# Sums of exponentials taken from a column of ones in v, in a two-layer attention kernel

## The chip, the cores and the metric

The kernel runs on one core of one Trainium2 chip. The metric is device time in microseconds, as the median of several runs. Engines are named as the profile names them: PE multiplies matrices, DVE, ACT and POOL work elementwise, SP only issues DMAs here; ACT and POOL can issue DMAs too.

## The reference

The input is x of shape (4, 32, 32, 768), in float32. Two layers follow one another, each with a residual: `x = x + layer(group_norm(x))`.

- Layer 0 makes q, k and v with three 768 x 768 products, splits them into 12 heads of 64 channels, and attends over the 1024 tokens of an image. Each score gets a bias for relative rows and one for relative columns, both from q. A projection follows.
- Layer 1 makes q, k and v likewise, then runs a 3x3 convolution per channel over each of them, and a layer norm over the 64 channels of a head, with a gain and an offset. Attention with the same kind of bias follows, q is added to its result, and a projection ends the layer.

```python
attn = softmax(q @ k.T * scale + rel_h + rel_w)   # per head, over 1024 keys
o = attn @ v                                      # layer 1: + q
```

The softmax divides by a sum of exponentials over the keys. How that sum is found in layer 1 is what changes. A layer norm's output, ahead of gain and offset, sums to zero over the 64 channels: the last channel is minus the sum of the other 63.

## The kernel before

All tensors lie with channels on the 128 partitions and tokens along the free axis. Two heads share the partitions (64 each) and are handled together as a *pair*; 6 pairs make one layer of one image, called a stage, and 8 stages (images 0 and 1 through layer 0, then through layer 1, then images 2 and 3 the same way) make 48 pairs. A pair's 1024 queries are handled in two *chunks* of 512 (`QC`).

**Attention of a chunk** (`attend`). The keys come in two groups of four tiles of 128. For each tile, PE makes the scores of both heads (L748) and adds the bias by a second product with `ones` (L750), ACT takes the exponential of 128 x 1024 values into `e` (L755). The four score tiles use the banks `ps_a`, `place_b`, `place_c` and `ps_a` again, so the fourth waits for the first one's exponential. After the group, PE multiplies the four `e` with v (`vt`) into `av`, 64 rows for each head (L770). On the side, DVE adds all eight `e` of a chunk into `acc` (L762 for the first two, L764 for the others).

When a chunk's last `av` is done, ACT copies it to SBUF as `weighed` (`copy`, L705). The remaining work is put off by a list, `rest`, and each call of `more()` runs one piece:

- `sums`: PE multiplies `acc` with a block of ones, which leaves each head's sums on all its 64 rows (`z`, L712); ACT copies them to `t` (L719) and finds a reciprocal by Ln and Exp (L721, L722). It comes after the next group's scores.
- `result`: DVE refines the reciprocal (L727, L728) and multiplies `weighed` by it (L731 in layer 1, where L732 applies v's gain and adds q; L734 in layer 0).
- `finish`: in layer 0 ACT adds v's bias.

**The other work** is laid between these groups. The generator `attend` yields 8 times for a chunk, two times after each group's scores and two times after each group's `av`, which makes 16 numbered *steps* for a pair, some 5 us each. A table, `events`, holds pieces of work by step number, written out by hand in `Pair.plan` and at the end of `two_layers`. No scheduler reorders them: each engine runs its instructions in the order in which the pieces were called.

For a pair of layer 1, whose pieces run while the pair before is attended, they are: products for q, k and v (`padded`, L131 `qkv`, with ACT's L515 into padded images), nine taps of the convolution on DVE (`taps`, L530 and L532), centring by a product (`centre`, `ln_c`) with ACT's squares and copies (L545, L546), sums of squares on DVE (`squares`, `lnv`), normalization (`norm`: `ln_ln` and `r_ln` on ACT, `t_ln` and L561 on DVE), transposes back (`back`, `ln_t`) with ACT's writes of `q`, `q_t` (L483, L484) and `k` (L492), and the bias: `positions` (`rel`, L590, copied to `whole` by L595 and L596), then `split`, in which ACT casts `whole` to `high` (L606), DVE takes the rest (L607), and POOL issues 16 DMAs of 128 KB that spread both into `bias` (L617).

In layer 0 most pairs use sevens of block products in place of eights (`sevens`, tiles `m4m2`, `m3m5`, `m1m6`, `m7`). They need sums of weight blocks, which `mix_weights(u)` makes once: it loads two weights by SP (the first of two steps), adds blocks on DVE and writes them to DRAM (`mixed`, the second step). For u of 12, 13 and 14, the projection of layer 1, the second step also finds the product of v's offset with the projection (`pbias`, L281: two groups of six products with a single column each). Token blocks are mixed on DVE by `mix_tokens` (L304). Group norm of the next stage (`gn_mean`, `gmean`, `gn_var`, xn) and the projection of the last one (`p4p2`, `p3p5`, `p1p6`, `p7`, `os_sums`) are further pieces.

**Banks.** `small_bank` gives one bank that all its users share in turn, and `bank` goes round a list (`turn`) of single banks in `place_b` and `place_c` and the small one, set anew after each group.

Of the kernel before, what the change touches and what calls it, by code (L numbers as in the profile page):

```python
# [17 lines left out]
P = 128  # L18
# [5 lines left out]
D = 64  # L24
HALF = T // 2
QC = 512
# [8 lines left out]
NSMALL = 81  # L35


IDENT, GROUP, CENTRE, HEADS, ONES = 0, P, 2 * P, 3 * P, 3 * P + 2
NCONST = 3 * P + 2 + D


LIMIT = 1e15
# [3 lines left out]
def two_layers(ctx: ExitStack, tc: tile.TileContext, keep, x_in, wqkv, wproj, rels, windows, vrow, small, const, onehot, picks, out):  # L46
# [19 lines left out]
    nc = tc.nc  # L66
# [5 lines left out]
    work = pool("work", 2)  # L72
# [52 lines left out]
    def small_bank(name):  # L125
        return ps_small.tile([P, 512], F32, tag="small", name=name)
# [14 lines left out]
    cst = fixed.tile([P, NCONST], F32, tag="cst", name="cst")  # L141
# [8 lines left out]
    def rsqrt(v, n, name):  # L150

        ln = stat.tile([P, n], F32, tag=f"ln{n}", name=f"ln_{name}")
        nc.scalar.activation(ln, v, AF.Ln)
        r = stat.tile([P, n], F32, tag=f"r{n}", name=f"r_{name}")
        nc.scalar.activation(r, ln, AF.Exp, scale=-0.5)
# [107 lines left out]
    def mix_weights(u):  # L263


        a = wp.tile([P, NC, P], F32, tag="wproj", name="mix_a")
        b = wp.tile([P, NC, P], F32, tag="wproj", name="mix_b")
        if u < PROJ_SUMS:
            (pa, sa), (pb, sb) = two(u, 0) if u < V_SUMS else two(2 * (u - V_SUMS), 2)
            nc.sync.dma_start(a, wqkv[0, pa, :, sa])  # L270
            nc.sync.dma_start(b, wqkv[0, pb, :, sb])
        else:
            layer, m = divmod(2 * (u - PROJ_SUMS), NC)
            for i, w in enumerate((a, b)):
                nc.sync.dma_start(w, wproj[layer, :, :, m + i, :].rearrange("h p q -> p h q"))
        yield
        for i, w in enumerate((a, b)):
            if u >= PROJ_SUMS and layer:
                ps = small_bank("pbias")
                for n in range(NC):  # L280
                    nc.tensor.matmul(ps[:, 0:1], w[:, n, :], col(LN + 5), start=(n == 0), stop=(n == NC - 1))  # L281
                nc.vector.tensor_tensor(pbias[:, m + i : m + i + 1], ps[:, 0:1], col(BIAS[1] + 18 + m + i), ALU.add)
# [24 lines left out]
    def group_norm(stage):  # L307

        xn = xns[stage]
        st = stat.tile([P, NC * 2, 6], F32, tag="bn", name="bn", bufs=1)  # L310
        for n in range(NC):
            for h in range(2):
                nc.vector.bn_stats(st[:, 2 * n + h, :], xn[:, n, h * HALF : (h + 1) * HALF])
            if n in (1, 3):
                yield
        mv = stat.tile([P, 2], F32, tag="mv", name="mv")
        nc.vector.bn_aggr(mv, st.rearrange("p a b -> p (a b)"))
        yield
# [5 lines left out]
        nc.vector.tensor_copy(mean, ps[:, 0:1])  # L324
        d = stat.tile([P, 1], F32, tag="gd", name="gd")
        nc.vector.tensor_sub(d, mv[:, 0:1], mean)
        nc.vector.scalar_tensor_tensor(d, d, d, mv[:, 1:2], ALU.mult, ALU.add)
        yield
        yield
        ps = small_bank("gn_var")  # L330
        nc.tensor.matmul(ps[:, 0:1], group, d, start=True, stop=True)
        v = stat.tile([P, 1], F32, tag="gv", name="gv")
        nc.vector.tensor_scalar(v, ps[:, 0:1], EPS, None, ALU.add)
        yield
        r = rsqrt(v, 1, "gn")
        yield
# [26 lines left out]
    class Pair:  # L363
# [189 lines left out]
        def norm(self, s):  # L553
            r = rsqrt(self.v, 2 * NKT, "ln")
            c = self.c[s].rearrange("p (a d) -> p a d", d=D)
            dst = c
            if s == 2:

                self.make_vt()
                dst = self.vt.rearrange("p t (j d) -> p (t j) d", d=D)  # L560
            nc.vector.tensor_tensor(dst, c, r.unsqueeze(2).to_broadcast([P, 2 * NKT, D]), ALU.mult)  # L561

        def back(self, s, h):

# [55 lines left out]
        def plan(self):  # L620

            Q, K, V = 0, 1, 2
            if not self.layer and not in_sevens(self.i):
                return [
                    (0, lambda: self.plain(Q, 0)),
                    (2, lambda: self.plain(Q, 1)),
                    (4, lambda: self.plain(K, 0)),
                    (5, lambda: self.positions(0)),
                    (6, lambda: self.plain(K, 1)),
                    (7, lambda: self.positions(1)),  # L630
                    (8, lambda: self.plain_v(0)),
                    (10, lambda: self.split()),
                    (10, lambda: self.plain_v(1)),
                ]
            if not self.layer:
# [51 lines left out]
    def attend(pair, os):  # L687
# [12 lines left out]
        for c in range(T // QC):  # L700
            cols = slice(c * QC, (c + 1) * QC)

            def copy(av):
                weighed = one.tile([P, QC], F32, tag="weighed", name="weighed")
                nc.scalar.copy(weighed, av)  # L705
                return weighed

            def sums(weighed, acc, c=c):

                z = small_bank("z")  # L710
                for j in range(2):
                    nc.tensor.matmul(  # L712
                        z[j * D : (j + 1) * D, :], cst[:, ONES : ONES + D], acc[:, j, :],
                        start=True, stop=True,
                    )
                at = 2 * (pair.i * (T // QC) + c)
                t = work.tile([P, QC], F32, tag="t", name="t", bufs=1)
                inv = work.tile([P, QC], F32, tag="inv", name="inv", bufs=1)
                nc.scalar.activation(t, z, AF.Copy, accum_out=seen[:, at : at + 1])  # L719

                nc.scalar.activation(inv, t, AF.Ln, bias=tiny)  # L721
                nc.scalar.activation(inv, inv, AF.Exp, scale=-1.0, accum_out=seen[:, at + 1 : at + 2])  # L722
                return weighed, t, inv
# [18 lines left out]
            for g in range(0, NKT, 4):  # L742
# [32 lines left out]
                more()  # L775
                if g + 4 == NKT:
                    rest.extend((sums, result, finish))
                    found = (copy(av), acc)
                yield
                yield  # L780

# [134 lines left out]

    for u, call, step in (
        (2, 0, 5), (7, 6, 11), (3, 13, 18), (4, 22, 29), (8, 31, 38), (5, 40, 47), (0, 49, 55), (6, 57, 63), (1, 65, 71),
        (9, 72, 77), (10, 78, 83), (11, 84, 89), (12, 138, 143), (13, 145, 150), (14, 152, 157),
    ):  # L920
        mix = mix_weights(u)
        for at_step in (call, step):
            at(at_step, lambda mix=mix: next(mix))
# [281 lines left out]
def _laid_out(inp):  # L1205
# [24 lines left out]
    const[:, CENTRE : CENTRE + P] = eye - head  # L1230
    const[:, HEADS : HEADS + 2] = np.kron(np.eye(2), np.full((D, 1), 1.0 / D))
    const[:, ONES : ONES + D] = 1.0
    key = np.arange(T)
    onehot = np.concatenate([np.arange(S)[:, None] == key // S, np.arange(S)[:, None] == key % S])

# [36 lines left out]
```

## Time and profile before

| | |
|---|---|
| time, median of 3 runs | 3917.45 us (3915.82 to 3919.93) |
| profiled execution, its time | 3920.75 us |
| its span, first to last instruction | 3918.9 us |
| mean granted PE clock | 0.993 |
| L764 and L762, adds into `acc` on DVE | 576 x 1225 ns and 96 x 1224 ns |
| L712, products for `z` on PE | 384 records, 103.6 us |
| L705, L719, L721, L722 on ACT | 96 each, 587, 600, 722 and 631 ns |
| L281, products for `pbias` on PE | 72 records, 12.4 us |
| DMA traffic | 318 MB, 81 GB/s in the mean |

A PE product in float32 shows as two records, each 128x512 one with its partner on the other 64 columns at the same time. Busy time is the union of the records. A line's idle time is that of its engine just before it, with the releaser that ended it. PEclk is the clock that PE was granted, as a share of full speed[...].

### The profile page before, as it was taken

The page shows a single profiled execution, that of the slowest core. Times are in us where ns is not written, and L with a number is a line of the kernel's source. Part 1 is how long each engine was busy: PE and PEld are TensorE (multiplying, and loading weights), DVE is VectorE, ACT ScalarE, POOL GpSimd, SP SyncE. Part 2 cuts the span into 40 slices and gives each one's busy share as a digit, 9 for nine tenths or more (in the row PEclk, how much of TensorE's full clock was granted, in tenths as well). Part 3 has the DMA queues.
Part 4 walks back from the last instruction along what each step waited for, and adds up shares of the span by engine and source line. Part 5 has one row for each costly group of instructions (what it writes and reads, how often), then busy time and mean ns, then how long its engine had stood idle before and what let it go on. Part 6 is the DMA issues. An engine that isn't in the chain of part 4 may idle for free.

```text
span 3918.9 us, 79880 instructions
## 1 busy us (share of the span) xinstructions
PE 3835.0 (98%) x34738; PEld 1726.2 (44%) x34738; DVE 2673.5 (68%) x3088; ACT 1850.3 (47%) x2741; POOL 411.7 (11%) x776
## 2 busy tenths in 40 slices
PE   7999999999999999999899999999999999999998
PEld 3535535534344444444444455355443444434442
DVE  2566454448789988799654554445686898878885
ACT  2455434445345553455533554254553555535551
POOL 0111000110000010000010010011100010000010
PEclk9999999999999999999999999999999999999999
DMA  4344452331331122311144222522115121142112
GB/s 147 102 120 120 127 163 61 94 83 38 105 100 39 39 60 83 115 45 39 41 118 135 56 73 64 167 63 75 42 52 155 35 56 43 39 118 57 36 47 95
DMA packets 184710, 318.11 MB, mean 81 GB/s; under 512 B 24352, under 2 KB 77472, under 8 KB 184352
## 3 DMA queue, kind: packets, MB, share of 16 engines
q1 hardware_dynamic: 122912, 212.19, 17.3%
q0 software_dynamic: 61440, 100.71, 11.2%
q8 instruction: 277, 4.54, 0.5%
q14 instruction: 81, 0.66, 0.1%
HBM read 172.23 MB, written 39.91 MB: 54 GB/s over the span
## 4 chain that ended last, share of the span: by engine, by line
PE 86%; DVE 11%; DMA 1%; issue 1%; ACT 1%; POOL 0%; DVEq 0%; SPq 0%; ACTq 0%
PE qkv L131 18%; PE s L748 15%; PE av L770 15%; PE m4m L131 4%; PE m3m L131 4%; PE m1m L131 4%; PE s L750 4%; DVE shared L532 3%; PE p3p L131 3%; DVE acc L764 3%; PE p1p L131 3%; PE p4p L131 3%; PE ln_c L131 3%; PE rel L590 3%; PE z L712 2%; PE m L131 2%
## 5 line engine op out<-in xcount | busy, mean ns | idle before, releaser
L755 ACT ACTIVATE e<-s 128x1024 f32<-128x1024 f32 x768 | 777.2, 1025 | 412.1 <-PE s L750 379.5
L764 DVE TENSOR_TENSOR acc<-acc,e 128x1024 f32<-128x1024 f32 x576 | 705.5, 1225 | 182.7 <-ACT e L755 132.2
L131 PE MATMUL qkv<-xn,wqkv_t 128*64 128x512 f32 x3648 | 815.8, 596 | 6.8 <-DVE gmean L324 4.1
L748 PE MATMUL s<-q,k 64*128 64x512 f32 x3072 | 817.1, 609 | 4.3 <-ACT e L755 3.5
L532 DVE SCALAR_TENSOR_TENSOR shared<-shared,sm 128x1056 f32<-128x1056 f32 x576 | 758.4, 1317 | 15.0
L750 PE MATMUL s<-bias,ones 64*128 64x512 f32 x1536 | 617.0, 796 | 10.9 <-DMA bias<-high 7.5
L770 PE MATMUL av<-e,vt 128*64 128x512 f32 x2624 | 595.0, 595 | 0.0
L617 POOL DMA_DIRECT2D bias<-high x384 | 203.6, 546 | 3237.8 <-ACT high L606 3003.6
L131 PEld LDWEIGHTS qkv<-xn,wqkv_t 128*64 128x64 f32 x3648 | 254.2, 137 | 491.5 <-issue 481.6
L515 ACT ACTIVATE shared<-qkv,sm 128x512 f32<-128x512 f32 (+1 forms) x288 | 129.3, 502 | 632.7 <-PE qkv L131 632.7
L748 PEld LDWEIGHTS s<-q,k 64*128 64x128 f32 x3072 | 283.2, 188 | 263.2 <-issue 216.8
L770 PEld LDWEIGHTS av<-e,vt 128*64 128x64 f32 x2624 | 185.6, 137 | 347.1 <-issue 322.0
L762 DVE TENSOR_TENSOR acc<-e 128x1024 f32<-128x1024 f32 x96 | 117.5, 1224 | 285.9 <-ACT e L755 280.1
L750 PEld LDWEIGHTS s<-bias,ones 64*128 64x128 f32 x1536 | 150.8, 189 | 199.2 <-issue 191.6
L617 POOL DMA_DIRECT2D bias<-whole x384 | 206.1, 558 | 106.6 <-DVE whole L607 97.0
L705 ACT COPY weighed<-av 128x512 f32<-128x512 f32 x96 | 56.4, 587 | 279.3 <-PE av L770 279.3
L131 PEld LDWEIGHTS ln_c<-cst,shared 128*64 128x64 f32 x2304 | 130.9, 137 | 48.5 <-issue 41.0
L590 PEld LDWEIGHTS rel<-q,rel 64*32 64x32 f32 x6144 | 111.7, 105 | 78.0 <-issue 58.7
L131 PE MATMUL ln_c<-cst,shared 128*64 128x128 f32 x2304 | 138.9, 273 | 6.4 <-DVE shared L532 5.7
L131 PE MATMUL m4m<-xn,wqkv_t 128*64 128x512 f32 x528 | 122.4, 599 | 4.0 <-issue 3.0
L400 DVE TENSOR_TENSOR shared<-shared,m3m 128x512 f32<-128x512 f32 x66 | 45.4, 687 | 118.3 <-PE m3m L131 118.2
L590 PE MATMUL rel<-q_t,rel 64*32 64x32 f32 x6144 | 123.3, 195 | 2.3 <-issue 2.3
(149 smaller groups left out, 4234.8 us busy)
## 6 DMA issues: line engine op xcount, KB each, us to landing
bias<-high POOLq DMA_DIRECT2D x384, 128.0 KB, 2.8
bias<-whole POOLq DMA_DIRECT2D x384, 128.0 KB, 3.0
wqkv_t<-in_wqkv SPq DMA_DIRECT2D x78, 384.0 KB, 3.1
wqkv_t<-mixed SPq DMA_DIRECT2D x66, 384.0 KB, 3.1
wproj_t<-mixed SPq DMA_DIRECT2D x48, 384.0 KB, 3.3
wqkv_t<-in_wqkv SPq DMA_DIRECT2D x66, 192.0 KB, 2.5
xn<-in_x SPq DMA_DIRECT2D x24, 512.0 KB, 7.8
x<-in_x SPq DMA_DIRECT2D x48, 256.0 KB, 3.1
```

The costliest lines, as they stand in the source:

```text
L131: nc.tensor.matmul(ps[lo : lo + D], a[:, lo : lo + D], b, start=start, stop=stop, **kw)
L515: nc.scalar.activation(self.pad[s][:, rows, there : there + src.shape[2]], src, AF.Identity, bias=col(self.column(s)))
L532: nc.vector.scalar_tensor_tensor(y, window, tap, y, ALU.mult, ALU.add)
L590: nc.tensor.matmul(ps[lo : lo + S, k * S : (k + 1) * S].rearrange("p (b c) -> p b c", b=2), rel[rows, 2 * self.layer + i, first : first + ...
L617: nc.gpsimd.dma_start(sets, some.unsqueeze(1).to_broadcast([D // 2, 2, QC]))
L712: nc.tensor.matmul(z[j * D : (j + 1) * D, :], cst[:, ONES : ONES + D], acc[:, j, :], start=True, stop=True,)
L748: nc.tensor.matmul(ps[:, j, :], k[rows, keys], q[rows, cols], start=True, stop=False)
L750: nc.tensor.matmul(ps[:, j, :], ones[rows, keys], bias[c][rows, kt // 2, :], start=False, stop=True,)
L755: nc.scalar.activation(e, ps, AF.Exp)
L762: nc.vector.tensor_tensor(acc, es[0], es[1], ALU.add)
L764: nc.vector.tensor_tensor(acc, acc, e, ALU.add)
L770: nc.tensor.matmul(av[j * D : (j + 1) * D, :], pair.vt[:, kt, j * D : (j + 1) * D], e[:, j, :], start=(kt == 0), stop=(kt == NKT - 1),)
```

## The change

- **Layer 1's sums.** `norm` overwrites the last channel of each head's v with ones. Row 63 and row 127 of `av` are then the sums of exponentials of the two heads. `copy` issues two DMAs from ACT that spread these rows over 64 partitions each, into `t`. In `sums`, PE multiplies `weighed` with a constant block, `WHOLE`, that keeps the first 63 rows of a head and puts minus their sum in the last; ACT copies that back to `weighed`, and a copy of `t` onto `inv` with an accumulator takes the place of the old copy from `z`. The adds into `acc` stay in layer 0 only.
- **`split` of pairs 0 and 1** comes at step 8 ahead of V's first half, not at step 10 after it.
- **`mix_weights`** of 12, 13 and 14 has its steps at (124, 135), (137, 147) and (149, 159), before (138, 143), (145, 150) and (152, 157). Its `pbias` products take `bank`, not `small_bank`.
- **Warm products.** The first stage's group norm issues five products of the identity with 384 columns between `gv` and `rsqrt`; nobody reads them.
- The constants grow from 450 to 578 columns.

```diff
@@ mix_weights
-                ps = small_bank("pbias")
+                ps = bank("pbias")
@@ group_norm
         nc.vector.tensor_scalar(v, ps[:, 0:1], EPS, None, ALU.add)
         yield
+        if stage == stages[0]:
+            ps = small_bank("warm")
+            for _ in range(5):
+                nc.tensor.matmul(ps[:, : 3 * P], ident, cst[:, : 3 * P], start=True, stop=True)
         r = rsqrt(v, 1, "gn")
@@ norm
+            if s == 2:
+                nc.vector.memset(dst[:, :, D - 1 :], 1.0)
@@ plan, first two pairs
+                    (8, lambda: self.split()),
                     (8, lambda: self.plain_v(0)),
-                    (10, lambda: self.split()),
                     (10, lambda: self.plain_v(1)),
@@ attend
             def copy(av):
                 weighed = one.tile([P, QC], F32, tag="weighed", name="weighed")
                 nc.scalar.copy(weighed, av)
-                return weighed
+                if not pair.layer:
+                    return weighed, acc
+                t = work.tile([P, QC], F32, tag="t", name="t", bufs=1)
+                for rows in heads:
+                    nc.scalar.dma_start(t[rows], weighed[rows.stop - 1 : rows.stop, :].unsqueeze(1).to_broadcast([1, D, QC]))
+                return weighed, t
-            def sums(weighed, acc, c=c):
+            def sums(weighed, of, c=c):
-                z = small_bank("z")
-                for j in range(2):
-                    nc.tensor.matmul(z[j * D : (j + 1) * D, :], cst[:, ONES : ONES + D], acc[:, j, :], start=True, stop=True)
+                z = small_bank("z" if not pair.layer else "whole")
...
-                nc.scalar.activation(t, z, AF.Copy, accum_out=seen[:, at : at + 1])
+                if pair.layer:
+                    t = of
+                    halves(z, cst[:, WHOLE : WHOLE + P], weighed)
+                    nc.scalar.copy(weighed, z)
+                    nc.scalar.activation(inv, t, AF.Copy, accum_out=seen[:, at : at + 1])
+                else:
...
@@ attend, after each group's scores
-                    acc = work.tile([P, 2, QC], F32, tag="acc", name="acc", bufs=1)
-                    nc.vector.tensor_tensor(acc, es[0], es[1], ALU.add)
-                for e in es[2 * (g == 0) :]:
-                    nc.vector.tensor_tensor(acc, acc, e, ALU.add)
+                if not pair.layer:
...
@@ events
-        (12, 138, 143), (13, 145, 150), (14, 152, 157),
+        (12, 124, 135), (13, 137, 147), (14, 149, 159),
```

More of the change, by code (lines that the diff above doesn't have):

```diff
@@ L35 @@
 NSMALL = 81
-IDENT, GROUP, CENTRE, HEADS, ONES = 0, P, 2 * P, 3 * P, 3 * P + 2
-NCONST = 3 * P + 2 + D
+IDENT, GROUP, CENTRE, HEADS, ONES, WHOLE = 0, P, 2 * P, 3 * P, 3 * P + 2, 3 * P + 2 + D
+NCONST = 4 * P + 2 + D
 LIMIT = 1e15
@@ L705, in copy @@
                 nc.scalar.copy(weighed, av)
-                return weighed
-            def sums(weighed, acc, c=c):
-                z = small_bank("z")
-                for j in range(2):
[L712 to L715, printed above, removed]
+                if not pair.layer:
[6 more added lines that the diff above has]
+                z = small_bank("z" if not pair.layer else "whole")
                 at = 2 * (pair.i * (T // QC) + c)
-                t = work.tile([P, QC], F32, tag="t", name="t", bufs=1)
                 inv = work.tile([P, QC], F32, tag="inv", name="inv", bufs=1)
-                nc.scalar.activation(t, z, AF.Copy, accum_out=seen[:, at : at + 1])
+                if pair.layer:
[4 more added lines that the diff above has]
+                else:
+                    t = work.tile([P, QC], F32, tag="t", name="t", bufs=1)
+                    for j, rows in enumerate(heads):
+                        nc.tensor.matmul(z[rows, :], cst[:, ONES : ONES + D], of[:, j, :], start=True, stop=True)
+                    nc.scalar.activation(t, z, AF.Copy, accum_out=seen[:, at : at + 1])
                 nc.scalar.activation(inv, t, AF.Ln, bias=tiny)
@@ L760, in attend @@
                     av = ps_av.tile([P, QC], F32, tag="av", name="av")
-                    acc = work.tile([P, 2, QC], F32, tag="acc", name="acc", bufs=1)
-                    nc.vector.tensor_tensor(acc, es[0], es[1], ALU.add)
-                for e in es[2 * (g == 0) :]:
-                    nc.vector.tensor_tensor(acc, acc, e, ALU.add)
+                if not pair.layer:
+                    if g == 0:
+                        acc = work.tile([P, 2, QC], F32, tag="acc", name="acc", bufs=1)
+                        nc.vector.tensor_tensor(acc, es[0], es[1], ALU.add)
+                    for e in es[2 * (g == 0) :]:
+                        nc.vector.tensor_tensor(acc, acc, e, ALU.add)
                 yield
@@ L777, in attend @@
                     rest.extend((sums, result, finish))
-                    found = (copy(av), acc)
+                    found = copy(av)
                 yield
@@ L918, in two_layers @@
         (2, 0, 5), (7, 6, 11), (3, 13, 18), (4, 22, 29), (8, 31, 38), (5, 40, 47), (0, 49, 55), (6, 57, 63), (1, 65, 71),
-        (9, 72, 77), (10, 78, 83), (11, 84, 89), (12, 138, 143), (13, 145, 150), (14, 152, 157),
+        (9, 72, 77), (10, 78, 83), (11, 84, 89), (12, 124, 135), (13, 137, 147), (14, 149, 159),
     ):
@@ L1232, in _laid_out @@
     const[:, ONES : ONES + D] = 1.0
+    whole = np.eye(D)
+    whole[:, -1] = -1.0
+    whole[-1, -1] = 0.0
+    const[:, WHOLE : WHOLE + P] = np.kron(np.eye(2), whole)
     key = np.arange(T)
```

## The prediction

> **What bounds the kernel now.** I read the page's busy times first, then PE's waits, then busy time and granted clock in stretches, then the timeline of single stretches.
>
> ```profile
> PE 3835.0 (98%) x34738; PEld 1726.2 (44%) x34738; DVE 2673.5 (68%) x3088; ACT 1850.3 (47%) x2741; POOL 411.7 (11%) x776
> ```
>
> PE is all but full, so removed DVE work gains only where PE stands idle or runs slowly. Idle time is 3918.9 - 3835.0 = 83.9 us: 18.2 us before the first product, 8.5 us of output after the last one, the rest single gaps. PE's waits name them (engine and line, releaser: total, times, longest):
>
> ```profile
> PE s L750 <- DMA bias<-high: 7.5, 3, 4.3
> PE m4m L131 <- issue: 6.0, 6, 3.0
> PE p1p L131 <- DVE os_sums L845: 5.8, 4, 1.5
> PE ln_c L131 <- DVE shared L532: 5.7, 2, 3.9
> PE rel L590 <- issue: 4.3, 2, 2.3
> PE qkv L131 <- DVE gmean L324: 4.1, 3, 1.4
> PE pbias L281 <- DVE pbias L282: 3.7, 3, 3.2
> PE s L748 <- ACT e L755: 3.5, 3, 1.2
> ```
>
> No one of them exceeds 8 us. But a gap costs more than itself, as stretches around the longest ones show (length, busy per engine, PEclk):
>
> ```profile
> core 0: us, PE busy (x) PEld busy (x) DVE busy (x) ACT busy (x) POOL busy (x), PEclk, DMA share, GB/s
> 56.00:68.00 12.00, 7.69 (x32) 3.68 (x34) 2.45 (x2) 4.63 (x5) 5.00 (x10) 0.86 0.70 170
> 698.00:722.00 24.00, 21.74 (x96) 11.57 (x94) 11.96 (x18) 8.60 (x13) 6.21 (x12) 0.79 0.51 140
> 744.00:760.00 16.00, 15.75 (x328) 9.23 (x326) 6.80 (x16) 8.75 (x14) 0.00 (x0) 0.89 0.36 114
> 786.00:802.00 16.00, 12.81 (x60) 6.95 (x58) 8.72 (x13) 3.89 (x5) 4.82 (x8) 0.79 0.62 166
> 1864.00:1920.00 56.00, 42.77 (x452) 19.60 (x450) 46.50 (x49) 27.09 (x39) 8.33 (x16) 0.91 0.20 46
> 3786.00:3822.00 36.00, 27.29 (x321) 14.13 (x310) 26.34 (x33) 19.64 (x30) 8.30 (x16) 0.86 0.26 60
> ```
>
> Loss of a stretch = idle + (1 - PEclk) x length: 4.3 + 1.7 = 6.0; 2.3 + 5.0 = 7.3; 0.3 + 1.7 = 2.0; 3.2 + 3.4 = 6.6; 13.2 + 5.0 = 18.2; 8.7 + 5.0 = 13.7. These 54 us are nearly all there is to win.
>
> [...]after the 4.3 us gap that ends at 61.3 the clock reads 0.50 from 62 to 64. Columns of 0.50 also follow the `pbias` products of one column each, with hardly any gap (752 to 754). [...]no ACT DMA is in this trace, so its issue is priced by SP's, 0.33 us in the median. [...]96 new DMAs x 128 KB = 12.6 MB on 318 MB.
>
> **The change part by part.** Layer 1 has 24 pairs of heads and 48 chunks.
>
> *Sums from ones.* Removed: 7 adds (L762, L764) a chunk, 336 x 1.225 = 411 us of DVE. Added on DVE: 24 memsets of 16 columns, 0.06 us by the nearest memset (L361), under 2 us. PE keeps two products of 512 columns per chunk (`whole` for `z`, L712, 1.08 us): nothing. ACT gets a copy (0.59) and a copy with accumulation in place of nothing (0.60 + 0.20 for the read), 1.4 us x 48 = 67 us, and two DMA issues a chunk.
>
> What the lighter DVE frees:
> - The `gmean` copies (4.1 us) stand in DVE's order behind taps that acc adds delay by 3.8 us: gone. The three `e` waits (3.5 us) come from ACT's `ln_ln` waiting for a late `lnv`: gone.
> - The four `p1p` waits (5.8 us) stay: at 1060 DVE had idled 5.75 us for ACT's `r_ln`, so the adds don't cause them.
> - 1864 to 1920 (layer 1's last pair before layer 0): the waits for taps (1.85), for K's normalization (1.7), for the mixing of tokens (`m4m`, 3.0) and for `m3m` (0.8) go, since DVE has 5.2 us and 3.8 us of adds right ahead of these. What is late next: `rel` waits 2.6 us for ACT's `q_t`, and ACT is now 1.3 us later there (1.4 more work after `z`), so 3.9; `k` 0.4; bias 1.5 instead of 2.9, because `whole` minus `high` no longer queues behind adds, but the 16 POOL issues stay; clock some 3 us instead of 5. Together 8.8 for 18.2: **-9.4**. Bounds -4 and -13.5.
> - 3786 to 3822 likewise: rel 2.0 + 1.3, k 0.4, bias 1.5, clock 3, together 8.2 for 13.7: **-5.5**. Bounds -2 and -9.5.
> - With the 7.6 us above (bounds 3.5 and 7.6): **-7.6**.
>
> What it adds as waits. Between the two chunks of a pair nothing lies between the last `av` and the next scores:
>
> ```profile
> 1853.73 0.59 ACT L705 COPY weighed<-av 128x512 f32<-128x512 f32 x1 [2.53 <-PE av L770]
> 1854.46 0.22 ACT L155 ACTIVATE r_ln<-ln_ln 128x16 f32<-128x16 f32 x1
> 1855.01 4.29 ACT L755 ACTIVATE e<-s 128x1024 f32<-128x1024 f32 x4 [0.33 <-PE s L750]
> 1856.98 1.02 PE L748 MATMUL s<-q,k 64*128 64x512 f32 x4
> ```
>
> The issues stand after the copy, ahead of `ln_ln`, `r_ln` and the four `e`. The fourth score reuses the first one's banks, so it waits for the first `e`, done at 1856.04. Slack is 0.33 us on ACT plus 0.94 us on PE = 1.27 us. Two issues of 0.33 us and a wait for the copy's end, 0.1 to 0.6, fit or nearly: 0 to 0.3 us x 24 chunks, I take **+2**, bounds 0 and +7. The other 24 chunks have 6 us of products in that place. ACT's copy of `whole` then waits for `t` to land. It is due 5.5 us after `av`; a 128 KB bias DMA lands in 2.8 us from an issue that comes at 1.5: hidden, with 1.2 us to spare, and behind it `rel` has 6 us more in all pairs but the two above. If both covers fail it costs what the landing is late.
>
> At the end `whole` waits only for the copy, so the 1.8 us wait of `z` for acc falls, but the reciprocal's chain (copy, landing, copy, Ln, Exp) ends 1.4 us later and `os_sums` hang on it: **+1.5**, bounds 0 and +3.
>
> *Split before V's first half* (pairs 0 and 1). ACT's cast moves from 51.2 to 46.9, and the 16 POOL issues and the landing with it: 4.3 us earlier, exactly the wait at 61.3. The half-clock spell after it goes too: **-6.0**, bounds -4 and -6.3. V's copies have over 3 us of idle ACT before them; pair 1's scores showed no bias wait, so nothing there.
>
> *Products with the bias of layer 1's projection moved, in turning banks.* Three steps move to 135, 147, 159, their loads on SP to 124, 137, 149, so that each has 10 steps to land (a step is some 5 us, a landing 3.1): nothing. Each then stands right after `av`, its two groups in different banks, not behind `gmean` or each other's evacuation: the idle 2.3 + 0.3 + 3.2 goes. A late DVE would now hold the third score, 3.7 us later, behind 2.5 us of bn_stats: covered. The 3 us of one-column products stay, and I leave each the middle stretch's spell of half clock, 3 x 1.76 = 5.3 us for 15.9: **-10.6**, bounds -5 and -15.
>
> *Five warm products* of 384 columns fill the 2.8 us before the first `qkv`. That one's first 24 records take 7.88 us, later ones 5.37[...]. 10 records of 0.33 us[...], starting at 16.8, end near 22.6, and 24 warm records then at 28.0 instead of 27.2: they cost what they save. With 64 KB more of constants ahead of x: **+0.7**, bounds -1 and +1.5.
>
> **Sum:** -9.4 - 5.5 - 7.6 + 2 + 1.5 - 6.0 - 10.6 + 0.7 = -34.9 us. The profiled execution took 3920.75 us (span 3918.9), 3.3 above the median; the difference is applied to the median: 3917.45 - 34.9 = 3882.5 us.
>
> **The rivals.** *Small gain:* the gaps close only where the chain is DVE's own. Stage ends keep their loss, ACT's lateness eating the relief, and the `pbias` wait moves to a score: -6.0 - 7.6 + 1.5 + 2 + 0.7 = -9.4 and some part of -10.6: 3898 to 3910, typically 3903. For it speaks that ACT's `rel` waits sit in both stage ends; against it that DVE is over 95% busy right there.
> *Slower:* ACT's issues hold it. Past 1.27 us every further us costs PE 24 us. From 1.27 + 35/24 = 2.7 us for the pair, 1.4 us each, the whole gain is gone; at 1.9 each it is 24 x 2.5 = 60 us, 3942. Against it: SP's 0.33, POOL's 0.55 us; for it: no ACT DMA was ever measured here, and a source of one partition neither.
> *The sums do not leave the path:* the adds never bounded PE at all; then only the moved steps count, -6.0 - 10.6 + 2 + 1.5 + 0.7 = -12.4, 3905; it lies inside the second case.
>
> **How the numbers follow.** Some 0.2% (8 us) is what a measurement of this kernel can tell from no change, so faster means under 3909.6. Forecast 0.78, small gain 0.14 (0.06 of it within 0.2%), slower by ACT 0.08. Faster 0.86, same 0.06, slower 0.08. All bounds at their good ends give 3864, at their bad ends about 3910; I take 3865 to 3908, which leaves out the ACT case and the edges.
>
> **What would show it.** DVE near 2264 us, ACT near 1917; no wait of PE for `gmean`, none for bias at 61; `ln_c` and `m4m` waits gone, `rel` waits longer; 56:68 at clock 1.00; `e` of a pair's second chunk starting 0.3 to 0.8 us later, with few PE waits for it. It is wrong if PE waits for `e` 24 times, or if ACT waits for DMA `t`.

## The result, and the profile after

The changed kernel takes 3928.58 us in the median of 9 runs (3926.25 to 3930.31); the kernel before, 3917.12 us (3914.54 to 3920.95, 9 runs). The ratio is 1.0029, 95% interval 1.0019 to 1.0039: slower by 11.5 us, where 34.9 us less were forecast. The profiled execution has a span of 3924.5 us at a mean clock of 0.992.

The page of the kernel after, busy times:

```profile
PE 3836.7 (98%) x34748; PEld 1720.4 (44%) x34748; DVE 2279.9 (58%) x2776; ACT 1864.0 (47%) x2789; POOL 412.2 (11%) x776
```

Its DMA view, two queues (packets, MB, share of 16 engines) and two kinds of DMA (KB each, median us to landing):

```profile
q0 software_dynamic: 61440, 100.71, 11.0%
q10 hardware_dynamic: 7680, 12.59, 5.9%
...
bias<-whole POOLq DMA_DIRECT2D x384, 128.0 KB, 3.1
...
t<-weighed ACTq DMA_DIRECT2D x96, 128.0 KB, 7.7
```

DVE lost 394 us, near the 409 that the forecast took off, and PE's busy time grew by 1.7 us. The new queue q10, that of the DMAs for `t`, is the surprise: with an eighth of q0's bytes it holds the DMA engines for over half of q0's time, and one of its DMAs lands in 7.7 us in the median (the time from issue to the signal that it is done), not in the 2.8 that the forecast took from `bias`.

PE's waits, kernel after (total, times, longest):

```profile
PE s L767 <- DMA bias<-whole: 16.6, 3, 9.3
...
PE rel L598 <- ACT q L488: 9.2, 2, 4.6
PE p4p L131 <- ACT os_sums L872: 6.7, 1, 6.7
PE s L767 <- DMA bias<-high: 6.5, 1, 6.5
PE p1p L131 <- DVE os_sums L864: 6.3, 4, 1.6
PE s L765 <- ACT k L497: 3.3, 2, 1.6
```

The waits for `gmean`, `pbias`, `ln_c` through `shared` and the bias wait at 61 us are gone. In their place stand six waits of over 4 us, three for `bias` and three for ACT. Where they lie, by busy time and clock in stretches of the kernel after (us; PE, PEld, DVE, ACT, POOL busy; PEclk; DMA share; GB/s):

```profile
52.00:64.00 12.00, 12.00 (x142) 8.56 (x140) 2.45 (x2) 5.27 (x6) 6.82 (x14) 1.00 0.81 203
...
720.00:740.00 20.00, 20.00 (x180) 9.71 (x179) 9.84 (x15) 7.80 (x9) 0.00 (x0) 0.91 0.41 129
775.00:795.00 20.00, 20.00 (x100) 9.21 (x98) 11.90 (x17) 7.97 (x12) 4.03 (x7) 0.91 0.65 184
1845.00:1895.00 50.00, 33.43 (x412) 17.30 (x410) 28.34 (x34) 29.48 (x45) 8.32 (x16) 0.80 0.28 48
1950.00:1970.00 20.00, 13.65 (x122) 8.47 (x120) 6.60 (x7) 5.44 (x8) 8.32 (x16) 0.83 0.73 156
3777.00:3820.00 43.00, 28.25 (x382) 14.98 (x380) 17.02 (x25) 25.97 (x41) 8.32 (x16) 0.80 0.33 56
```

With the forecast's own measure, idle plus (1 - PEclk) x length: the start lost 6.0 us before and loses nothing; two of the `pbias` stretches lose 1.8 us each and the third, at 677, nothing, 3.6 instead of 15.9. But the first stage end loses 16.6 + 10.0 = 26.6 us (18.2 before), the second 14.8 + 8.6 = 23.4 (13.7 before), and 1950 to 1970, the start of the next pair, 6.4 + 3.4 = 9.8. There PE had waited 0.3 us for `bias` in the kernel before; the kernel after is shown second:

```profile
1972.97 0.50 PE L750 MATMUL s<-bias,ones 64*128 64x512 f32 x2 [0.32 <-DMA bias<-high]
...
1962.10 0.80 PE L767 MATMUL s<-bias,ones 64*128 64x512 f32 x2 [6.35 <-DMA bias<-whole]
```

This measure is rough. In the kernel before a record of a score product (L748) takes 1.06 us in the median at PEclk 0.50 (62 to 64.5) and 0.59 at 1.00 (66 to 70), 1.8 times as long where the measure counts 2, and where PE stands idle at half clock the measure books the time one and a half times. From 1874 to 1876 in the kernel after PE does nothing and PEclk reads 0.50, which makes 3 us of 2:

```profile
1874.00:1876.00 2.00, 0.00 (x0) 0.00 (x0) 1.97 (x2) 0.00 (x0) 0.00 (x0) 0.50 0.95 154
```

The times at which PE comes to the same piece of work don't depend on it. In us from the start of the profiled execution:

| PE is ready for | before | after | lead of the kernel after |
|---|---|---|---|
| `rel` at the first stage end | 1865.6 | 1846.0 | 19.6 |
| the next pair's first score | 1971.5 | 1954.6 | 16.9 |
| that pair's first `m4m` | 1977.6 | 1968.4 | 9.2 |
| `rel` at the second stage end | 3785.0 | 3777.8 | 7.2 |
| the last pair's second group of scores | 3821.6 | 3820.8 | 0.9 |
| the end of its last product | 3910.4 | 3916.7 | -6.3 |

So the kernel after is well ahead at the first stage end, and the loss lies at and behind it.

ACT's part in it, from its timeline in the kernel after (start, length; in brackets idle time and releaser):

```profile
1834.65 1.12 ACTq L719 DMA_DIRECT2D t<-weighed  x2
...
1843.53 0.58 ACT L730 COPY weighed<-whole 128x512 f32<-128x512 f32 x1 [3.59 <-DMA t<-weighed]
...
1948.78 1.04 ACT L614 CAST high<-whole 128x1024 fp32r<-128x1024 f32 x1 [1.32 <-issue]
...
3856.66 0.58 ACT L730 COPY weighed<-whole 128x512 f32<-128x512 f32 x1 [8.91 <-DMA t<-weighed]
...
3859.28 0.56 ACT L872 COPY os_sums<-p4p 128x512 f32<-128x512 f32 x1
```

The copy of `whole` waits for the landing, since the DMAs read the tile that it writes. At 1843.53 it is 3.6 us late, and the squares, `q` and `q_t` behind it by as much, so PE waits 4.6 us at `rel`. At 3856.66 it is 8.9 us late, and `os_sums` behind it costs PE 6.7 us. Before 1948.78 the two issues of `t` stand right ahead of `high`, whose bias DMAs then share the engines with them. The wait at 1955.75 isn't due to `t` alone: weight loads that SP issues from 1952.1 on come in between, and the engines move 258 to 290 GB/s from 1955 to 1961. At the same place `many_rows` (below), whose DMAs for `t` land in 2.4 us, still waits 2.1 us.

### The profile page after: what moved, and what is told of

It reads as the page before. It is cut to its first block, busy times and chain, and to the rows that moved or that the text cites. A ratio compares the mean times of both kernels' runs of the same rounds, so it can differ in the third digit from the quotient of the medians.

```text
span 3924.5 us, 79555 instructions
## 1 busy us (share of the span) xinstructions
PE 3836.7 (98%) x34748; PEld 1720.4 (44%) x34748; DVE 2279.9 (58%) x2776; ACT 1864.0 (47%) x2789; POOL 412.2 (11%) x776
## 4 chain that ended last, share of the span: by engine, by line
PE 88%; DMA 5%; ACT 3%; DVE 2%; issue 1%; ACTq 0%; POOL 0%; SPq 0%; DVEq 0%
PE qkv L131 18%; PE av L789 16%; PE s L765 15%; PE m4m L131 4%; PE m3m L131 4%; PE m1m L131 4%; PE s L767 4%; DMA t<-weighed 4%; PE p3p L131 3%; PE rel L598 3%; PE p4p L131 3%; PE p1p L131 3%; PE ln_c L131 2%; PE m L131 2%; PE z L735 1%; PE p L131 1%
## 5 line engine op out<-in xcount | busy, mean ns | idle before, releaser
L772 ACT ACTIVATE e<-s 128x1024 f32<-128x1024 f32 x768 | 769.2, 1023 | 414.5 <-PE s L767 385.3
L767 PE MATMUL s<-bias,ones 64*128 64x512 f32 x1536 | 618.2, 797 | 23.1 <-DMA bias<-whole 16.6
L783 DVE TENSOR_TENSOR acc<-acc,e 128x1024 f32<-128x1024 f32 x288 | 352.9, 1225 | 122.0 <-ACT e L772 96.5
L157 DVE TENSOR_TENSOR t_ln<-r_ln 128x16 f32<-128x16 f32 x72 | 12.6, 175 | 367.7 <-ACT r_ln L155 367.7
L781 DVE TENSOR_TENSOR acc<-e 128x1024 f32<-128x1024 f32 x48 | 58.8, 1225 | 226.9 <-ACT e L772 218.2
L598 PE MATMUL rel<-q,rel 64*32 64x32 f32 x6144 | 124.5, 196 | 10.2 <-ACT q L488 9.2
L744 DVE SCALAR_TENSOR_TENSOR t<-t,inv 128x512 f32<-128x512 f32 x96 | 65.7, 685 | 114.0 <-ACT inv L739 114.0
```

The source lines that it names most:

```text
L598: nc.tensor.matmul(ps[lo : lo + S, k * S : (k + 1) * S].rearrange("p (b c) -> p b c", b=2), rel[rows, 2 * self.layer + i, first : first + ...
L744: nc.vector.scalar_tensor_tensor(t, t, -1.0, inv, ALU.mult, ALU.mult)
L767: nc.tensor.matmul(ps[:, j, :], ones[rows, keys], bias[c][rows, kt // 2, :], start=False, stop=True,)
L772: nc.scalar.activation(e, ps, AF.Exp)
```

## The experiments

All ratios are to the kernel before, run beside them. Its medians lie between 3916.9 and 3918.6 us there, so a difference between two changed kernels of different sets is good to 1.7 us. The theory: **the landing of `t`** costs the time, in two ways: ACT waits for it in order, and it takes DMA engines from `bias`. Rivals: ACT's added work and issues; the moved steps; the order around `bias`.

**The two halves of the change.** `moved_only` has the moves of `split`, `pbias` and the warm products on the kernel before; `sums_only` has the ones alone.

```diff
# all edits are against the kernel after, and cut ("..."); sums_only:
-                ps = bank("pbias")
+                ps = small_bank("pbias")
...
-                    (8, lambda: self.split()),
                     (8, lambda: self.plain_v(0)),
+                    (10, lambda: self.split()),
...
-        (12, 124, 135), (13, 137, 147), (14, 149, 159),
+        (12, 138, 143), (13, 145, 150), (14, 152, 157),
...
-        if stage == stages[0]:
-            ps = small_bank("warm")
-            for _ in range(5):
-                nc.tensor.matmul(ps[:, : 3 * P], ident, cst[:, : 3 * P], start=True, stop=True)
```

> The kernel before with the moved steps alone (split ahead of V's first half, the three steps with the bias of layer 1's projection in turning banks at 135, 147, 159, five warm products); sums in layer 1 from acc as before. Landing theory (the loss comes from the DMAs that spread the sums): the moved steps keep what the prediction gave them, -6.0 - 10.6 + 0.7 = -16, so about 3901 us, ratio 0.996. ACT theory (the loss is ACT's added work and its issues): the same. Moved-steps theory (the loss comes from the moves): 3917 us or more, ratio 1.000 to 1.004.

> The changed kernel with the moved steps undone: only the sums from ones. Landing theory and ACT theory: 11.5 us of loss plus the 16 us that the moves no longer give, about 3945 us, ratio 1.007; PE waits over 6 us for bias and for os_sums at the three places where the changed kernel shows them. Moved-steps theory: 3917 us or less.

Measured: `moved_only` 3902.0 us, ratio 0.9955 (0.9941 to 0.9969), 16.1 us less; `sums_only` 3952.06 us (3939.91 to 3955.63), ratio 1.0086 (1.0072 to 1.0100), with nearly the same longest waits for bias (9.2 us), `rel` (4.6) and `os_sums` (6.7) as the kernel after. The moves gain what they were summed to gain, and the ones lose. On top of the ones the moves gain 23.5 us, 7.4 more than alone. This rest stays open: the clock of `sums_only` is 0.988 to 0.991 over its runs, and its profile is of the fastest of them (3939.91 us), 12 us under the median.

**Without the DMA, and with another source.** In `no_dma` ACT makes `t` from the product; `many_rows` keeps DMAs, bytes and place, but reads 64 partitions. In both, and in the kernels below that read other rows, `t` doesn't hold the sums: what the engines have to do is kept, the result is not.

```diff
# no_dma
...
-                for rows in heads:
-                    nc.scalar.dma_start(t[rows], weighed[rows.stop - 1 : rows.stop, :].unsqueeze(1).to_broadcast([1, D, QC]))
...
+                    t = work.tile([P, QC], F32, tag="t", name="t", bufs=1)
...
-                    nc.scalar.activation(inv, t, AF.Copy, accum_out=seen[:, at : at + 1])
+                    nc.scalar.activation(t, z, AF.Square, accum_out=seen[:, at : at + 1])
# many_rows
-                    nc.scalar.dma_start(t[rows], weighed[rows.stop - 1 : rows.stop, :].unsqueeze(1).to_broadcast([1, D, QC]))
+                    nc.scalar.dma_start(t[rows], weighed[rows])
...
```

> The changed kernel without the DMAs that spread the sums: ACT takes t from the product of `whole` instead (a square, so that it is positive), with the same number of ACT operations; the sums are thus not used, and the output is another. Landing theory: no ACT wait for t; the bias waits of 9.3, 6.4 and 6.5 us fall to 3 us or less each, the wait for os_sums through ACT falls from 6.7 to under 2; about 3890 us (3882 to 3896), ratio 0.993. ACT theory in its form 'ACT's added copies': they are all still here, so only the two issues (1.1 us a chunk) go, 3920 us or more. Order theory (bias is late because the steps around it moved, not because the DMAs share the engines): the bias waits stay, 22 us of them, and the time is 3905 to 3915 us.

> The changed kernel with the same DMAs in number, size and place (64 rows of 2 KB each from ACT), but row i is read from partition i instead of all 64 from one partition; t then does not hold the sums (it is squared ahead of the logarithm), and the output is another. If the landing of 7.7 us is due to one partition being read: it falls to about 3 us, ACT waits for t fall from 92 us to under 10, bias waits fall to 3 us or less, about 3890 us, ratio 0.993. If it is due to the number of rows or bytes, or to ACT's queue: landing stays at 7 us or more and the time at about 3928 us, ratio 1.003.

Measured: `no_dma` 3873.23 us, ratio 0.9885 (0.9870 to 0.9900); `many_rows` 3884.83 us, ratio 0.9912 (0.9896 to 0.9927). `no_dma` is 9 us below the range that was expected, `many_rows` 5 below its figure; why the gain is larger stays open. From the page of `many_rows`:

```profile
q10 hardware_dynamic: 7680, 12.59, 1.3%
```

The same packets and bytes take 1.3% of the engines instead of 5.9%; the landing is 2.4 us in the median, ACT waits for `t` once (3.0 us), and bias waits sum to 7.0 us instead of 23.1. With every issue and every ACT operation still there, 43.7 us come back, so neither is what loses; the issues are worth at most the 11.6 us between the two kernels. The order rival falls too: `many_rows` has all moves, and its longest bias wait is 3.5 us, that of the kernel before 4.3.

How the reads go shows best in a short stretch right behind two issues, of the kernel after:

```profile
1249.00:1251.00 2.00, 1.88 (x12) 0.62 (x8) 1.83 (x7) 2.00 (x3) 0.00 (x0) 1.00 0.85 26
1251.00:1253.00 2.00, 2.00 (x24) 1.27 (x24) 1.97 (x3) 1.56 (x2) 0.00 (x0) 1.00 0.84 59
```

and of `many_rows`:

```profile
1249.00:1251.00 2.00, 1.88 (x12) 0.87 (x10) 1.35 (x9) 1.94 (x6) 0.00 (x0) 1.00 0.55 120
1251.00:1253.00 2.00, 2.00 (x13) 0.64 (x10) 1.97 (x3) 2.00 (x3) 0.00 (x0) 1.00 0.00 0
```

The last two columns, read together: in the first stretch the engines of the kernel after are busy to 85% and move 26 GB/s, those of `many_rows` are busy to 55% and move 120. Of these DMAs only the source differs between the two kernels, so it is the source that makes busy engines move so little.

**Another queue.**

```diff
# from_sp
-                    nc.scalar.dma_start(t[rows], weighed[rows.stop - 1 : rows.stop, :].unsqueeze(1).to_broadcast([1, D, QC]))
+                    nc.sync.dma_start(t[rows], weighed[rows.stop - 1 : rows.stop, :].unsqueeze(1).to_broadcast([1, D, QC]))
```

> The changed kernel with the DMAs of t issued from SP instead of ACT. Landing theory: landing stays at 7 us or more, ACT still waits for t about 90 us in all and bias is late by as much; only ACT's hold of 1.1 us goes, which PE sees at the two k waits (1.6 to 0.4): 3922 to 3929 us, ratio 1.001 to 1.003. Rival (ACT's queue or its issue makes them slow): landing near 3 us, 3885 to 3895 us.

Measured: 3925.1 us, ratio 1.0020 (1.0012 to 1.0028). The landing is 7.8 us, ACT waits 101.3 us for `t`, bias waits reach 10.6 us; the `k` waits fall from 1.6 us to 0.4. So it isn't ACT's queue that makes the landing late. ACT's issues cost some 3 us (3.5 between the medians, 2.4 in the `k` waits); the intervals of the two ratios overlap, so this is a rough size only.

**The partitions or the engines.** `four_rows` and `four_ports` read four partitions of each head, 16 times each: 60 to 63 of its 64, or 3, 7, 11 and 15. If the number of engines sets the time, both are equally slow; if the choice of partitions does (the port theory of the second expectation), `four_ports` is faster.

```diff
# four_rows
+                    nc.scalar.dma_start(t[rows], weighed[rows.stop - 4 : rows.stop, :].unsqueeze(1).to_broadcast([4, D // 4, QC]))
...
# four_ports
+                    nc.scalar.dma_start(t[rows], weighed[rows.start + 3 : rows.start + 16 : 4, :].unsqueeze(1).to_broadcast([4, D // 4, QC]))
...
```

> As many_rows, but each head's DMA reads four partitions, each 16 times, instead of 64 partitions once (many_rows) or one partition 64 times (the changed kernel). If reads of one partition go one after the other, the landing falls in proportion to the reads of one partition: from 3.0 and 7.7 us, 0.075 us a read, so about 4.2 us here, the queue's share near 2.5%, and the time 3887 to 3895 us. If a repeated read as such is slow (or any source under some number of partitions), landing stays near 7.7 and the time near 3928 us.

> As four_rows (each head's DMA reads four partitions 16 times each; t does not hold the sums and is squared), but the partitions are 3, 7, 11 and 15 of each head[...]. Engine theory (four source rows put the DMA on four engines, and these bound it): ACT comes to t as late as in four_rows, 11 us after the first issue, and the time is 4010 to 4020 us. Port theory[...]: a row takes half as long or less, as in many_rows (0.13 us by its queue's 1.3% share, against 0.26 us in four_rows), so 32 rows an engine take some 4.2 us and not 8.3; t is there some 6 to 7 us after the issue, the queue's share is near 1.3%, and the time 3890 to 3930 us.

Measured: `four_rows` 4018.51 us, ratio 1.0262 (1.0246 to 1.0278); `four_ports` 3887.03 us, ratio 0.9921 (0.9905 to 0.9938). `four_rows` was expected at 3887 to 3895 if the reads of one partition queue up, or near 3928 if a repeated read as such is slow; it is slower than both. There ACT waits 171.0 us for `t`, and PE 51.4 us in 20 waits at the transposes `ln_t` behind it (1.3 us in the kernel after): the landing is now too late inside the loop as well. `four_ports` is 3 us below the range of the port theory. Right behind the issues, `four_rows`:

```profile
1260.00:1262.00 2.00, 1.88 (x12) 0.65 (x10) 1.86 (x7) 2.00 (x3) 0.00 (x0) 1.00 0.23 25
1262.00:1264.00 2.00, 2.00 (x28) 1.43 (x28) 1.97 (x2) 1.24 (x2) 0.00 (x0) 1.00 0.22 25
```

and `four_ports`:

```profile
1250.00:1252.00 2.00, 1.88 (x12) 0.84 (x10) 1.31 (x9) 1.94 (x6) 0.00 (x0) 1.00 0.26 88
1252.00:1254.00 2.00, 2.00 (x12) 0.63 (x12) 1.97 (x3) 2.00 (x3) 0.00 (x0) 1.00 0.11 43
```

Both keep about a quarter of the 16 engines busy in the first of the two stretches (0.23 and 0.26), where the kernel after has 0.85 and `many_rows` 0.55. The rate there differs by more than three: 25 GB/s from partitions 60 to 63 of each head, 88 from 3, 7, 11 and 15. From its one partition of each head the kernel after lands a DMA of 128 KB in 6.3 us in the best case and 7.7 in the median.

What is shown is that the choice of the four partitions decides, at the same number of engines, rows and repeats. What sets the two choices apart is not shown: the port of the expectation was the author's guess, and no run reads four partitions at other places.

**Which of the two ways, and where.** `later` leaves the DMAs and calls `sums` one slot later; `spread_later` issues the DMAs one slot later and `sums` two behind `av`, with the last pair's sums from acc; `ends_only` reads 64 partitions in pairs 22, 23, 46 and 47 alone.

```diff
# later
+            def held(weighed, t):
...
+                return weighed, t
...
-                    rest.extend((sums, result, finish))
+                    rest.extend((held, sums, result) if pair.layer and pair.i < len(items) - 1 else (sums, result, finish))
# spread_later
...
+            def spread(weighed, _):
...
+                    rest.extend((spread, sums, result) if pair.ones else (sums, result, finish))
# ends_only
+ENDS = (22, 23, 46, 47)
...
+                    if pair.i in ENDS:
+                        nc.scalar.dma_start(t[rows], weighed[rows])
...
```

> The changed kernel, with layer 1's `sums` (the product, ACT's copies, logarithm and exponential) called one slot later, so that ACT comes to `t` some 10 us after the issue instead of 5; the DMAs are issued where they were, the last pair is left as it is. Landing theory, half of it: ACT's waits for t (92 us) all but vanish, rel's two waits of 4.6 us fall to about 0.9; but the DMAs still share the engines with bias, so the bias waits of 9.3, 6.4 and 6.5 us stay: about 3917 us (3910 to 3921), ratio 1.000. Rival (bias is late because ACT, held by t, casts `high` late): the bias waits fall too, 3890 to 3900 us.

> The changed kernel with the DMAs of t issued one slot later, behind the first four exponentials of the next chunk, and `sums` two slots after `av`; the last pair takes its sums from acc as before. Landing theory: the DMAs land beside products and clear of the bias DMAs, so ACT's waits for t, the bias waits and the wait for os_sums go: 3885 to 3893 us, ratio 0.992 to 0.994. Rival (the DMAs cost by their engine time wherever they stand): bias or other loads are late in other places, 3905 us or more.

> The changed kernel, with the DMAs read from 64 partitions in pairs 22, 23, 46 and 47 alone (8 chunks of 48; there t does not hold the sums and is squared, so the output is another); the other 40 chunks read one partition. Landing theory with the place that the trace gives (the late landing costs only where the cover of qkv products is missing): nearly all of many_rows' gain comes back, 3885 to 3893 us, ratio 0.992 to 0.994. Rival (the 40 others cost too, by engine time and ACT's waits of 3.3 us): half or more of the 44 us stays, 3907 us or more.

Measured: `later` 3915.91 us, ratio 1.000 (0.9991 to 1.0008); `spread_later` 3912.78, ratio 0.9989 (0.9983 to 0.9996); `ends_only` 3892.11, ratio 0.9935 (0.9921 to 0.9948). PE's waits in `later`:

```profile
PE s L771 <- DMA bias<-whole: 20.6, 4, 9.1
...
PE p4p L131 <- ACT os_sums L876: 6.7, 1, 6.7
```

`rel`'s waits for ACT are gone and 12.7 us with them, the bias waits are not: they sum to 20.6 us, where the kernel after has 23.1 and `many_rows` 7.0. So what these DMAs take of the engines is a cost of its own, and not a late cast of `high`. The wait for `os_sums` stays because `later` leaves the last pair as it was. `ends_only` gives back 36.5 of 43.7 us with 8 chunks of 48: the other 40 still make ACT wait 74.4 us, but PE's longest wait for ACT in that kernel is 1.6 us: the late landing is hidden behind other products.

`spread_later` missed its 3885 to 3893 us. At the stage ends, with no `qkv` between, the product that `sums` needs is done 4.4 us after the issue, and `t` is there only after 8.9:

```profile
1874.55 1.12 ACTq L724 DMA_DIRECT2D t<-weighed  x2
1883.40 0.59 ACT L735 COPY weighed<-whole 128x512 f32<-128x512 f32 x1 [7.83 <-DMA t<-weighed]
...
1886.03 2.83 ACT L777 ACTIVATE e<-s 128x1024 f32<-128x1024 f32 x3
```

That is ACT's timeline in `spread_later`: the bias waits have fallen to 3.3 us or less, but now the exponentials stand behind the wait. PE waits 4.7 us for `e` at either stage end and 5.2 for `whole` behind the first of them; the other 16 waits for `e` are 0.5 us each.

**A version without the DMA.** If the ones go into channel 0, the one product can give the spread sum in 63 rows of each head and the restored channel in the row of channel 0; only that row is to be swapped with the sum that `weighed` holds. `product_act` does all four copies of a row on ACT, `product_mixed` gives two to DVE.

```diff
# product_mixed
-                nc.vector.memset(dst[:, :, D - 1 :], 1.0)
+                nc.vector.memset(dst[:, :, :1], 1.0)
...
-                    nc.scalar.copy(weighed, z)
-                    nc.scalar.activation(inv, t, AF.Copy, accum_out=seen[:, at : at + 1])
+                    nc.scalar.activation(t, z, AF.Copy, accum_out=seen[:, at : at + 1])
+                    for rows in heads:
+                        lost = slice(rows.start, rows.start + 1)
+                        nc.scalar.copy(t[lost], weighed[lost])
+                        nc.vector.tensor_copy(weighed[lost], z[lost])
...
-    whole = np.eye(D)
-    whole[:, -1] = -1.0
-    whole[-1, -1] = 0.0
+    whole = np.zeros((D, D))
+    whole[0] = 1.0
+    whole[:, 0] = -1.0
+    whole[0, 0] = 0.0
```

> No DMA for t: the ones go into channel 0, and the one product after av gives the sum in 63 rows of each head and minus the sum of the other channels in the row of channel 0; ACT copies the product to t and swaps that row (four copies of one row by 512, 0.6 us each, in place of one copy of all rows). PE's work is that of the changed kernel. Landing theory: no wait for t, bias on time, time that of no_dma (3873 us) plus 1.8 us of ACT's chain at two stage ends and the end, 3875 to 3884 us, ratio 0.990 to 0.992. Rival (ACT's chain is what holds): 1.8 us more in every chunk's chain shows as PE waits for e, k and q, 3890 us or more.

> As product_act, but the two copies from the product's bank into weighed are DVE's, so ACT's chain is only 0.6 us longer than in no_dma. Landing theory: 3873 to 3880 us, ratio 0.989 to 0.991. Rival (the bank is held by a late DVE and the next user of it, rel or a projection product, waits): PE waits for DVE weighed, over 1 us each in many chunks, 3885 us or more.

Measured: `product_act` 3881.81 us, ratio 0.9904 (0.9889 to 0.9919); `product_mixed` 3878.63 us (3874.83 to 3881.43), ratio 0.9900 (0.9885 to 0.9916). Both make the true sums, and both beat the kernel before by 1% and the kernel after by more. They lie in the ranges that were expected. Stretches at the stage ends of `product_mixed`:

```profile
1840.00:1890.00 50.00, 41.08 (x470) 19.74 (x468) 33.79 (x41) 30.53 (x44) 8.30 (x16) 1.00 0.22 55
1930.00:1950.00 20.00, 20.00 (x200) 12.42 (x198) 8.53 (x10) 9.16 (x14) 8.31 (x16) 1.00 0.62 153
3750.00:3795.00 45.00, 41.07 (x347) 18.97 (x334) 29.21 (x45) 33.51 (x49) 8.30 (x16) 1.00 0.20 48
```

They lose 8.9, 0 and 3.9 us, with the clock at 1.00 in all three. ACT's longer chain shows where it was expected, in `rel`'s waits at the two stage ends: 0.7 us the longest in `no_dma`, 1.5 in `product_mixed`, 2.8 in `product_act`. `product_mixed` has two more kinds of wait: 3.7 us in two for DVE's `t_ln`, and one of 1.9 for `e`.

## Why the prediction was wrong

- **The step that failed: the landing of `t`**, called "hidden, with 1.2 us to spare" since "a 128 KB bias DMA lands in 2.8 us". It measures 7.7 us in the median, some 5 more. The size was the same, the source was not: a DMA for `bias` reads 32 partitions, one for `t` reads one. With a source of 64 partitions and the same DMAs otherwise the kernel takes 3884.8 us (`many_rows`), 2.3 from the forecast; its stage ends lose 13.2 and 5.4 us, together 1.6 more than forecast. The text did say that no DMA from one partition was measured, but only as an argument for slow issues.
- **"If both covers fail it costs what the landing is late"** was right, and the two pairs without cover were named; but that cost entered neither the sum nor the range, nor a rival. At the stage ends -9.4 and -5.5 were forecast (losses of 8.8 and 8.2 us); measured by the same rule, 26.6 and 23.4. Most of it is the landing, by `ends_only`.
- **Bias at the stage ends, "1.5 instead of 2.9"**: 9.3 and 6.5 us. And a wait that no step held, 6.4 us at 1955.75. The forecast weighed 12.6 MB against 318 MB; the engines' time was what counted, 5.9% beside q0's 11.0%, and all of a chunk's within some 7 us. `later` shows that these waits stand without ACT's.
- **The end, +1.5**: the stretch that holds the last products of layer 1 lost 4.9 + 1.9 = 6.8 us before and loses 11.2 + 3.6 = 14.9 after. The chain was named (landing, then `os_sums`), the landing again mis-sized. The kernel before, then the one after:

```profile
3822.00:3870.00 48.00, 43.10 (x200) 15.54 (x198) 35.62 (x48) 18.33 (x25) 0.00 (x0) 0.96 0.11 35
...
3820.00:3872.00 52.00, 40.76 (x186) 14.37 (x184) 21.64 (x35) 18.64 (x29) 0.00 (x0) 0.93 0.27 35
```

- **How far this accounts for the miss.** By the leads of the table above, the first stage end loses 2.7 us where 9.4 were to be gained, the next pair 7.7 where nothing was said, the second stage end 6.3 where 5.5 were to be gained, and the end 7.2 where 1.5 were to be lost. These four are 12.1 + 7.7 + 11.8 + 5.7 = 37 us off, of the 34.9 + 6.3 = 41 between the forecast and the two profiled executions. By the forecast's own "loss of a stretch" they would be 17.8 + 15.2 + 9.5 + 6.6 = 49, more than the whole miss, since it counts idle time at half clock too high.
- **ACT's issues, +2 (0 to 7)**: an issue takes 0.50 us in the median, not 0.33, and ACT goes on 1.20 us after the copy. The slack of 1.27 us held: PE's waits for `e` sum to 0.7 us. What the issues cost shows elsewhere, in the `k` waits of 1.6 us, 0.4 without issue: 2.4 us. That this is near the +2 is luck, but the rival that had the issues hold ACT is refuted.
- **ACT's added work** was read wrongly. The forecast had "a copy with accumulation in place of nothing", but it takes the place of the old one from `z`, so one copy of 0.59 us is added for a chunk, 28 us in all and not 67. ACT's busy time rose by 13.7 us, to 1864.0 and not 1917, and where `t` lands early, ACT is 0.6 us later at `rel` and not 1.3 (PE waits up to 0.9 us for `q` in `many_rows`, up to 0.3 before).
- **The moves** were right in their sum, -6.0 - 10.6 + 0.7 = -15.9, and -16.1 measured alone, with luck in the parts. In the kernel after, by the forecast's measure, the early `split` gives the 6.0 us and the `pbias` steps 12.3 instead of 10.6. Behind the warm products PE comes to its first `rel` 2.1 us later than before (39.52 and 37.46), where 0.7 was forecast; 0.8 of it lies ahead of them, in a later `gn_mean`. The `qkv` products that follow take 15.6 us up to that `rel` instead of 18.1: a record takes 0.64 us at most, before up to 1.12, with PEclk at 1.00 in both. But the ten warm records take 6.3 us. The `gmean` waits and nearly all of those for `e` went, and the `p1p` waits stayed, as said.
- The mark that was set for being wrong, "ACT waits for DMA `t`", is what the trace shows: 92.2 us in 25 waits.

## What to carry to other kernels

Price a DMA by the partitions that it reads, not by its bytes or by another DMA of the same size (no run here varied the side that is written). Here a row spread over 64 partitions landed in 7.7 us, 64 rows of 64 partitions in 2.4, and of the engines' time the one took 5.9%, the other 1.3%; PE's waits for `bias` sum to 23.1 us beside 7.0. Where a new wait is hidden in most of the loop, work out its price in the few places without cover and put that in the sum: here 8 chunks of 48 decided the sign. Before moving data between partitions by DMA, see whether a matrix product that is made anyway can do it.

## What the runs showed of the hardware

Engine time for one row of 2 KB, from the queue's share x 16 x span over 96 x 64 rows: 0.60 us from one partition of each head, 0.26 from four side by side (60 to 63), 0.13 from 64, 0.09 from four that stand apart (3, 7, 11 and 15). The queue's lines of `four_rows` and `four_ports`; those of the other two stand above:

```profile
q10 hardware_dynamic: 6528, 12.58, 2.5%
...
q10 hardware_dynamic: 6528, 12.58, 0.9%
```

So `four_rows`, with a quarter of the engines, holds less engine time in all than the kernel after, 2.5% against 5.9%, yet its transfer ends later: `t` is there some 11 us after the first issue in `four_rows`, some 9 in the kernel after. Other transfers aren't better off: PE stands idle for 26.5 us ahead of its products with `bias` in `four_rows`, for 23.1 in the kernel after. In `four_ports` a DMA with four source rows used a quarter of the engines as well (0.26) and still landed early enough, but for one wait of 4.8 us.
